# First stage of a two-layer SSM and mixture-of-experts kernel: one stored row per token, a skewed loop over pairs of tiles, and three engines in written order

## The chip, the cores and the metric

The kernel runs on one core of one Trainium2 chip. The metric is the device time of one launch in microseconds; the kernel before took 2048.63 us, the median of three runs from 2046.37 to 2051.86. The profile is that of one more execution, taken by the hardware profiler. Its engines are TensorE (PE, with its weight loads as PEld), VectorE (DVE), ScalarE (ACT), GpSimd (POOL) and SyncE (SP, which here only issues DMAs).

## The reference

The input `x` has 8 sequences of 1024 tokens of width 256, all in float32. Two layers follow, each of the form "x plus mixer of the normalized x plus experts of the normalized x":

```python
xn = layernorm(x)
x = x + attn0(xn) + ffn0(xn)      # attn0: scan h = A h + B x_t, y = C h + D x, layernorm, gelu, @ W_out.T + b_out, + xn
xn = layernorm(x)
x = x + attn1(xn) + ffn1(xn)      # attn1: softmax over an axis of length one; ffn1: 8 experts with a capacity

# ffn0, for each token
scores = sigmoid(xn @ router_weight.T)                 # 8 experts in 2 groups
masked = (scores + correction_bias) in the better group, 0 elsewhere
e1, e2 = top 2 of masked;  w1, w2 = scores[e1], scores[e2], divided by their sum
routed = w1 * expert_e1(xn) + w2 * expert_e2(xn)       # (silu(xn @ gate) * (xn @ up)) @ down, inner width 128
shared = (silu(xn @ sw_gate) * (xn @ sw_up)) @ sw_down
ffn0 = routed + shared
```

The change concerns the normalization, the shared expert and the routing of the first layer, and the rows that its routed experts read and write.

## The kernel before, in words

The 8192 tokens are 64 tiles of 128 tokens (one token per partition), 8 tiles per sequence. All of `x` lies in SBUF in the tile `y`. The program is written in a tile framework: a planner orders the instructions of every engine from dependencies, written order and modelled times, and adds the waits. Each engine then runs its own queue strictly in the planned order.

**First stage.** It goes over pairs of tiles, 32 pairs, in five sets of 8, 16, 16, 16 and 8 tiles. For a set, `scale` (L556) takes the square root of the variances on ScalarE (another activation table than the sigmoid's) and makes `rstd`, `off` and `up` on VectorE. For each tile, `measure` (L550) takes mean and variance on VectorE, one set ahead, and `normal` (L571) writes the normalized rows into `xr4` on VectorE, a ring of three buffers of four tiles each. After every fourth tile, two DMAs store these rows in DRAM, in `xnd`, which has **two rows per token**, one for each of its two experts: 256 values and, in column 256, the gate of that choice.

For each pair, `shared` (L596) lets TensorE turn the rows (`pair_turned`, four transposes, L249, copied by ScalarE at L253), makes the router's products (L606), and computes the shared expert: `hidden` (gate and up products, L263; sigmoid on ScalarE, L268; two products on VectorE, L270 and L271) and `down` (L278). `both` (L586) makes on ScalarE the copy `xc` for the scan (L588) and x plus xn in place in `y` (L592). VectorE adds the shared result to `y` (L617). In before all of one pair is written one after the other. Two steps of `krylov(0)`, which makes powers of the scan's matrix for four groups of channels (`begin`, then seven `level`; L322 on TensorE, copies L329 and L333), are written behind each pair until its eight steps are done.

Per sequence, `fill` (L533) writes the bias `b_out` into the DRAM tensor `base` from SP, and a DMA of POOL then accumulates `y` into it (L655). After every second sequence, `route0` (L482) makes the routing of 16 tiles: 33 small VectorE instructions one after the other, and two DMAs that store the gates (L528).

**After it.** A short part counts each expert's tokens (L671 to L724). Then come the scan and, woven into it, `find`/`found` (which token stands where in the experts' lists) and 71 expert blocks of 256 rows: `bring` gathers rows of `xnd` by an indirect DMA and the weights, `widen` turns them and computes `hidden`, `narrow` (L806) computes `down`, scales each row by its gate (L811) and scatters it into `yr`, two rows per token. The next part reads `base` and both `yr` rows of each token and adds them (`load`, L942), projects, normalizes, and makes the second layer, whose experts fill the second half of the time.

These lines set the first stage's order in before:

```python
for k in range(0, len(g), 2):
    for i in g[k + 4 : k + 6]:
        normal(i, ...)
    for i in nxt[k * len(nxt) // len(g) : (k + 2) * len(nxt) // len(g)]:
        measure(i, ...)
    ...
    shared(i, pr, rstd[:, k : k + 2])
    for step in steps[:2]:
        step()
```

Of the kernel before, what the change touches and what calls it, by code (L numbers as in the profile page):

```python
# [9 lines left out]
F32 = mybir.dt.float32  # L10
# [8 lines left out]
P = 128  # L19
EPS = 1e-5  # L20
BIG = 3.0e38


@with_exitstack
def kernel(
# [47 lines left out]
    NCOL = NBLK * BLK // P  # L73
    XW = D + 8
# [10 lines left out]
    kscr = dram.tile([D, 2 * P], F32, name="kscr")  # L85
    base = dram.tile([NTOK, D], F32, name="base")

    xnd = dram.tile([2 * NTOK, D + 1], F32, name="xnd")
# [109 lines left out]
    def pick_two(pool, v, n, hot, val):  # L198


        for k in range(2):
# [6 lines left out]
            nc.vector.tensor_reduce(first, cand, AX.X, ALU.max)  # L208
            oh = hot[k]
            nc.vector.tensor_tensor(oh, cand, bc(first, 2, [P, n, E]), ALU.is_equal)  # L210
            if k == 0:
                rest = pool.tile([P, n, E], F32, name="rest")
                nc.vector.scalar_tensor_tensor(rest, oh, -BIG, v, ALU.mult, ALU.add)
                v = rest


    with tc.tile_pool(name="xpool", bufs=1) as xpool, tc.tile_pool(name="mo", bufs=2) as mo, tc.tile_pool(
# [12 lines left out]
        g0 = xpool.tile([P, 2, NT], F32, name="g0")  # L230
        up = xpool.tile([P, NT], F32, name="up")
        off = xpool.tile([P, NT], F32, name="off")
# [4 lines left out]

        choice = xpool.tile([P, NCOL], I32, name="choice")
        goes = xpool.tile([P, NCOL], I32, name="goes")
# [16 lines left out]
        def hidden(xT, wb, pgu=None):  # L256
# [10 lines left out]
            sg = mo.tile([P, 2 * P], F32, name="sg")  # L267
            nc.scalar.activation(sg, pgu[:, 0, :], AF.Sigmoid)  # L268
            hh = mo.tile([P, 2 * P], F32, name="hh")
            nc.vector.tensor_tensor(hh, pgu[:, 0, :], sg, ALU.mult)  # L270
# [183 lines left out]
        with tc.tile_pool(name="sh", bufs=1) as sh, tc.tile_pool(name="ld", bufs=2) as ld, tc.tile_pool(  # L454
# [5 lines left out]
            scores = sh.tile([P, NT, E], F32, name="scores")  # L460
            cb_t = sh.tile([P, E], F32, name="cb_t")
# [10 lines left out]
            bout_t = sh.tile([P, D], F32, name="bout_t")  # L472
            nc.scalar.dma_start(bout_t, b_out.partition_broadcast(P))
# [6 lines left out]
            nc.vector.tensor_copy(rwT.rearrange("p c e -> p (c e)"), pr[:, : DC * E])  # L480

            def route0(n, tiles):  # L482
# [8 lines left out]
                nc.vector.tensor_tensor(lo, v[:, :, 0:2], v[:, :, 2:4], ALU.min)  # L491
                gs = rt.tile([P, 2 * n], F32, name="gs")
                nc.vector.tensor_reduce(gs, lo, AX.X, ALU.max)
                top = rt.tile([P, 2 * n], F32, name="top")
                nc.vector.tensor_reduce(top, hi, AX.X, ALU.min)
                nc.vector.tensor_tensor(gs, gs, top, ALU.max)
                nc.vector.tensor_reduce(top, hi, AX.X, ALU.max)
                nc.vector.tensor_tensor(gs, gs, top, ALU.add)
                gs2 = gs.rearrange("p (t g) -> p t g", g=2)
                gm = rt.tile([P, n, 2], F32, name="gm")  # L500
                nc.vector.tensor_tensor(gm[:, :, 0], gs2[:, :, 0], gs2[:, :, 1], ALU.is_ge)
                nc.vector.tensor_tensor(gm[:, :, 1], gs2[:, :, 1], gs2[:, :, 0], ALU.is_gt)
                masked = rt.tile([P, n, E], F32, name="masked")
# [7 lines left out]
                pick_two(rt, masked, n, hot, [rt.tile([P, n], F32, name=f"top{j}") for j in range(2)])  # L511
                w = rt.tile([P, n, E], F32, name="w")
                nc.vector.tensor_tensor(hot0[:, tiles, :], hot[0], hot[1], ALU.add)
                nc.vector.tensor_copy(first0[:, tiles, :], hot[0])
                nc.vector.tensor_tensor(w, hot0[:, tiles, :], sc, ALU.mult)
                den = rt.tile([P, n], F32, name="den")
                nc.vector.tensor_reduce(den, w, AX.X, ALU.add)
                nc.vector.tensor_scalar(den, den, 1e-20, None, ALU.add)
                nc.vector.reciprocal(den, den)
                nc.vector.tensor_tensor(w, w, bc(den, 2, [P, n, E]), ALU.mult)  # L520
                for k in range(2):
                    wk = rt.tile([P, n, E], F32, name="wk")
                    nc.vector.tensor_tensor(wk, w, hot[k], ALU.mult)
                    nc.vector.tensor_reduce(g0[:, k, tiles], wk, AX.X, ALU.add)
                    mine = xnd[2 * tiles.start * P : 2 * tiles.stop * P, :].rearrange(
                        "(i p k) c -> k p i c", p=P, k=2
                    )[k]
                    nc.sync.dma_start(mine[:, :, D], g0[:, k, tiles])  # L528
# [4 lines left out]
            def fill(b):  # L533

                nc.sync.dma_start(
                    base[b * S : (b + 1) * S, :].rearrange("(i p) d -> p i d", p=P),
                    bc(bout_t, 1, [P, TPB, D]),
                )

# [31 lines left out]
            def normal(i, mv, rstd):  # L571
# [7 lines left out]
                if i % 4 == 3:  # L579
                    for kk in range(2):  # L580
                        mine = xnd[2 * (i - 3) * P : 2 * (i + 1) * P, :].rearrange(
                            "(i p k) c -> k p i c", p=P, k=2
                        )[kk]
                        nc.sync.dma_start(mine[:, :, :D], rows[i // 4])
# [10 lines left out]

            def shared(i, pr, rstd):  # L596


                n = i // 2
                pt = None  # L600
                if n % 3:
                    pt = ps_m.tile([P, 512], F32, name="pm").rearrange("p (c t) -> p c t", c=DC)
                xT = pair_turned(rows[i // 4][:, i % 4 : i % 4 + 2, :], pt)
# [11 lines left out]
                pgu = ps_k.tile([P, 2, 2 * P], F32, name="pk") if n % 2 else None  # L615
                pd = down(hidden(xT, sw, pgu), sw)
                nc.vector.tensor_tensor(y[:, i : i + 2, :], pd, y[:, i : i + 2, :], ALU.add)  # L617

# [7 lines left out]
            pr = None  # L626
            for s, g in enumerate(sets):
                mv = mvs[s]
                rstd = scale(g, mv)
                nxt = []  # L630
                if s + 1 < len(sets):
                    nxt = list(sets[s + 1])
                    mvs.append(ld.tile([P, len(nxt), 2], F32, name="mv"))
                for i in g[:4]:
                    normal(i, mv[:, i - g[0], 0:1], rstd[:, i - g[0] : i - g[0] + 1])
                for k in range(0, len(g), 2):
                    for i in g[k + 4 : k + 6]:
                        normal(i, mv[:, i - g[0], 0:1], rstd[:, i - g[0] : i - g[0] + 1])
                    for i in nxt[k * len(nxt) // len(g) : (k + 2) * len(nxt) // len(g)]:
                        measure(i, mvs[s + 1][:, i - nxt[0], :])  # L640
                    i = g[k]
                    if i % TPB == 0:
                        pr = ps_y.tile([P, TPB, E], F32, name="py")
                        fill(i // TPB)
                        if i // TPB >= NB - len(pack):
                            nc.sync.dma_start(*pack[i // TPB - NB + len(pack)])
                    shared(i, pr, rstd[:, k : k + 2])
                    for step in steps[:2]:
                        step()
                    steps = steps[2:]  # L650
                    if i % TPB == TPB - 2:
                        b = i // TPB
                        tiles = slice(b * TPB, (b + 1) * TPB)
                        nc.scalar.activation(scores[:, tiles, :], pr, AF.Sigmoid)
                        nc.gpsimd.dma_start(  # L655
                            base[b * S : (b + 1) * S, :].rearrange("(i p) d -> p i d", p=P),
                            y[:, tiles, :], accum_op=ALU.add,
                        )
# [807 lines left out]
```

## Time and profile before

| | us |
|---|---|
| median of the runs | 2048.63 |
| profiled execution | 2030.81 |
| its span in the trace | 2029.1 |
| TensorE busy | 1825.1 |
| VectorE busy | 697.3 |
| ScalarE busy | 716.2 |
| GpSimd busy | 670.8 |
| mean granted TensorE clock | 0.952 of full speed |

The page's slices cut the span into 40 equal parts of about 51 us. A digit is the busy share in tenths, PEclk the clock granted to TensorE in tenths of full speed, DMA the mean busy share of the 16 DMA engines. In a list in order of time, a row begins with start and duration in us; "x8" means that eight instructions are merged; a bracket tells how long the engine was idle before and what released it. In a list of waits the numbers are the total in us, how many times, and the longest.

### The profile page before, as it was taken

To read this page: it belongs to the slowest core of one execution; us is meant where nothing else is said; L and a number is where in the kernel's file an instruction comes from. 1 tells how busy PE (TensorE), PEld (TensorE's weight loads), DVE (VectorE), ACT (ScalarE), POOL (GpSimd) and SP (SyncE) were. 2 spreads that over 40 slices of the span, in tenths; PEclk is the share of its full clock that TensorE was granted. 3 is DMA by queue.
4 is the path that set the end of the run, shared out by engine and by line. 5 is a ranking of instruction groups with operands and counts; after the bars stand their busy time and mean duration, and the time that the engine had idled before them with its cause. 6 is when DMAs were issued, how large, how long until landed. Compare 5 with 4: busy or idle time off the path is not lost.

```text
span 2029.1 us, 24196 instructions
## 1 busy us (share of the span) xinstructions
PE 1825.1 (90%) x8619; PEld 1379.9 (68%) x8619; DVE 697.3 (34%) x2101; ACT 716.2 (35%) x1626; POOL 670.8 (33%) x680
## 2 busy tenths in 40 slices
PE   6988798989898888748995999999999999999996
PEld 5866576877777776537973666666666666666664
DVE  6764795444453434437775111001000110001010
ACT  5963353232222222337982222222222222222221
POOL 0000002555555546411112333333333333333312
PEclk9988899999999999868997999999999999999998
DMA  9999313555454545499995223232323222232211
GB/s 267 222 199 201 49 54 115 151 149 152 146 164 138 146 130 170 122 281 253 224 237 128 38 60 61 42 72 39 82 39 73 41 61 57 57 59 38 40 18 21
DMA packets 228888, 233.16 MB, mean 115 GB/s; under 512 B 50904, under 2 KB 203296, under 8 KB 228640
## 3 DMA queue, kind: packets, MB, share of 16 engines
q0 software_dynamic: 69408, 102.87, 26.2%
q1 hardware_dynamic: 156672, 126.35, 22.5%
q10 hardware_dynamic: 2688, 2.40, 0.4%
q8 instruction: 68, 1.11, 0.2%
q14 instruction: 52, 0.43, 0.1%
HBM read 136.87 MB, written 97.85 MB: 116 GB/s over the span
## 4 chain that ended last, share of the span: by engine, by line
PE 48%; DMA 4%; issue 2%; DVE 2%; ACT 1%; POOL 1%; POOLq 0%; SPq 0%; DVEq 0%; ACTq 0%
PE phe L1393 22%; PE poe L1411 21%; DMA hb<-yr 2%; PE px L1376 1%; PE pd L996 1%; PE pd L1061 1%; DMA hb<-base 1%; PE pt L933 1%; DMA out_dram<-yo,invi 1%; PE pi L1162 0%; PE pt L1206 0%; PE pt L1042 0%; DVE y L1003 0%; DVE st L178 0%; POOL out_dram L1085 0%
## 5 line engine op out<-in xcount | busy, mean ns | idle before, releaser
L1393 PE MATMUL phe<-xTe,w1t 128*128 128x512 f32 x1024 | 447.1, 595 | 0.6 <-issue 0.6
L1411 PE MATMUL poe<-w2t,hT 128*128 128x256 f32 x2048 | 447.3, 379 | 0.0
L1411 PEld LDWEIGHTS poe<-w2t,hT 128*128 128x128 f32 x2048 | 386.7, 190 | 51.7 <-issue 0.5
L1393 PEld LDWEIGHTS phe<-xTe,w1t 128*128 128x128 f32 x1024 | 195.4, 191 | 233.6 <-issue 230.5
L1423 POOL DMA_INDIRECT out_dram<-yo,invi x128 | 201.6, 1575 | 447.7 <-DMA out_dram<-yo,invi 257.2
L1400 ACT ACTIVATE hT<-phe,b1T 128x512 f32<-128x512 f32 x256 | 175.9, 687 | 248.3 <-PE phe L1393 241.4
L1422 ACT ACTIVATE yo<-yo,gr 128x256 f32<-128x256 f32 x128 | 58.0, 500 | 441.4 <-DVE yo L1418 441.4
L1418 DVE TENSOR_TENSOR yo<-poe,b2t 128x512 f32<-128x512 f32 x64 | 44.2, 691 | 406.6 <-PE poe L1411 406.6
L1362 POOL DMA_INDIRECT xg<-xd,invi x128 | 124.0, 969 | 163.8 <-PE px L1376 125.8
L322 PE MATMUL pk<-kr 128*128 128x129 f32 (+7 forms) x896 | 151.4, 306 | 29.4 <-ACT kr L333 23.8
L1377 DVE COPY xTe<-px 128x512 f32<-128x512 f32 x64 | 41.2, 685 | 383.3 <-PE px L1376 383.2
L322 PEld LDWEIGHTS pk<-kr 128*128 128x128 f32 x896 | 130.1, 202 | 52.9 <-ACT kr L333 34.5
L814 POOL DMA_INDIRECT yr<-yo,goes x142 | 140.7, 990 | 76.7 <-DVE yo L811 35.2
L792 POOL DMA_INDIRECT xb<-xnd,choice x142 | 139.1, 980 | 46.9 <-issue 33.5
L263 PE MATMUL pgu<-xT,wb 128*128 128x256 f32 x568 | 144.2, 399 | 8.9 <-ACT xT L253 7.6
L263 PEld LDWEIGHTS pgu<-xT,wb 128*128 128x128 f32 x568 | 110.3, 200 | 37.4 <-ACT xT L253 18.5
L333 ACT COPY kr<-pk 128x256 f32<-128x256 f32 x192 | 69.6, 374 | 123.4 <-DVE kr L329 103.5
L268 ACT ACTIVATE sg<-pgu 128x256 f32<-128x256 f32 x87 | 33.3, 383 | 199.7 <-PE pgu L263 139.3
L278 PE MATMUL pd<-wb,hh 128*128 128x256 f32 x284 | 86.4, 421 | 11.4 <-DVE hh L271 7.6
L787 POOL COPY wb<-wrow 1x1 int32<-1x1 int32 x71 | 12.8, 180 | 234.4 <-PE pgu L752 117.5
L270 DVE TENSOR_TENSOR hh<-pgu,sg 128x256 f32<-128x256 f32 x87 | 36.8, 423 | 138.8 <-ACT sg L268 116.1
L996 PE MATMUL pd<-woutT,gT 128*128 128x256 f32 x256 | 63.5, 404 | 22.1 <-DVE y L1003 22.1
(322 smaller groups left out, 2375.3 us busy)
## 6 DMA issues: line engine op xcount, KB each, us to landing
wb<-wpk SPq DMA_DIRECT2D x71, 384.0 KB
xnd<-xr SPq DMA_DIRECT2D x32, 512.0 KB
hk<-kscr SPq DMA_DIRECT2D x32, 512.0 KB
hb<-yr POOLq DMA_DIRECT2D x14, 1024.0 KB
base<-bout_t SPq DMA_DIRECT2D x8, 1024.0 KB
base<-y POOLq DMA_DIRECT2D x8, 1024.0 KB
hb<-base SPq DMA_DIRECT2D x8, 1024.0 KB
w1t<-in_L_ffn_w_dram SPq DMA_DIRECT2D x8, 1024.0 KB
```

What stands on the lines that cost most here:

```text
L263: nc.tensor.matmul(pgu[:, j, :], lhsT=gu[:, j, c, :], rhs=xT[:, c, :], start=(c == 0), stop=(c == DC - 1),)
L278: nc.tensor.matmul(pd[:, q, :], lhsT=hh[:, q * P : (q + 1) * P], rhs=wb[:, 2 * DC * I : WW], start=True, stop=True,)
L322: nc.tensor.matmul(pk[:, j, :n], lhsT=t[:, 1 - j, P:], rhs=t[:, j, P - k : P - k + n], start=True, stop=True,)
L333: nc.scalar.copy(t[:, :, P:], pk[:, :, k : k + P])
L792: nc.gpsimd.indirect_dma_start(out=xb[:, q, : D + 1], out_offset=None, in_=xnd[:, :], in_offset=bass.IndirectOffsetOnAxis(ap=choice[:, 2 * ...
L814: nc.gpsimd.indirect_dma_start(out=next(yr_own)[:, :], out_offset=bass.IndirectOffsetOnAxis(ap=goes[:, 2 * n + q : 2 * n + q + 1], axis=0) ...
L996: nc.tensor.matmul(po[:, q, :], lhsT=gT[:, c, (t + q) * P : (t + q + 1) * P], rhs=woutT[:, c, :], start=(c == 0), stop=(c == DC - 1),)
L1362: nc.gpsimd.indirect_dma_start(out=xg[:, q, :], out_offset=None, in_=xd[:, :], in_offset=bass.IndirectOffsetOnAxis(ap=invi[:, q0 + q : q0 ...
L1393: nc.tensor.matmul(ph, lhsT=w1t[:, c, h * P : (h + 1) * P], rhs=xT[:, c], start=(c == 0), stop=(c == DC - 1),)
L1400: nc.scalar.activation(hT[:, h], ph, AF.Relu, bias=b1T[:, e * HC + h : e * HC + h + 1])
L1411: nc.tensor.matmul(po[:, r, :], lhsT=hT[:, h, q + r, :], rhs=w2t[:, h, :], start=(h == 0), stop=(h == HC - 1),)
L1423: nc.gpsimd.indirect_dma_start(out=of[:, :], out_offset=bass.IndirectOffsetOnAxis(ap=invi[:, q0 + r : q0 + r + 1], axis=0), in_=yo[:, r, : ...
```

## The change

It has five parts.

1. `xnd` has one row per token, of 258 values: the normalized row and both gates (`XR = D + 2`). One DMA instead of two stores four tiles of rows, and one instead of two the gates. The list `choice` holds token numbers, and a new tile `which` holds for each place of the lists a 1 at the choice that it is.
2. `base` is written once, from SP, with `y` after the shared result has been added, four tiles at a time; the fills and the accumulating DMAs are gone. The bias is loaded once, halved (`bhalf`), and added in `narrow` to both expert rows of each token; `narrow` picks the gate with `which`.
3. Pairs are skewed: the next pair is turned before the current one's router and hidden products, and `down` and the add of a pair come behind the hidden products of the next one. One Krylov step is written behind every second pair.
4. `route0` is a generator of 13 pieces, three of which are written behind each pair; it is called for 16, 16, 16, 8 and 8 tiles.
5. The loop stands in a block in which TensorE, VectorE and ScalarE keep the written order. `begin(s + 1)`, the scale of the next set and its first four `normal`, is written at the last pair of a set.

`hidden` also writes the sigmoid straight into `hh`, which has three buffers.

```diff
-    xnd = dram.tile([2 * NTOK, D + 1], F32, name="xnd")
+    xnd = dram.tile([NTOK, XR], F32, name="xnd")
...
+        bhalf = xpool.tile([P, D], F32, name="bhalf")
+        nc.scalar.dma_start(bhalf, b_out.partition_broadcast(P))
+        nc.scalar.mul(bhalf, bhalf, 0.5)
...
-            sg = mo.tile([P, 2 * P], F32, name="sg")
-            nc.scalar.activation(sg, pgu[:, 0, :], AF.Sigmoid)
-            hh = mo.tile([P, 2 * P], F32, name="hh")
-            nc.vector.tensor_tensor(hh, pgu[:, 0, :], sg, ALU.mult)
+            hh = mo.tile([P, 2 * P], F32, name="hh", bufs=3)
+            nc.scalar.activation(hh, pgu[:, 0, :], AF.Sigmoid)
+            nc.vector.tensor_tensor(hh, pgu[:, 0, :], hh, ALU.mult)
...
-                    for kk in range(2):
-                        mine = xnd[2 * (i - 3) * P : 2 * (i + 1) * P, :].rearrange(
-                            "(i p k) c -> k p i c", p=P, k=2
-                        )[kk]
-                        nc.sync.dma_start(mine[:, :, :D], rows[i // 4])
+                    mine = token_rows(slice(i - 3, i + 1))
+                    nc.sync.dma_start(mine[:, :, :D], rows[i // 4])
...
+                if i % TPB == TPB - 2:
+                    nc.scalar.activation(
+                        scores[:, i - TPB + 2 : i + 2, :], pr, AF.Sigmoid
+                    )
+                pgu = ps_k.tile([P, 2, 2 * P], F32, name="pk") if i // 2 % 2 else None
+                return hidden(xT, sw, pgu)
+
+            def add_shared(i, hh):
+
+                pd = down(hh, sw)
                 nc.vector.tensor_tensor(y[:, i : i + 2, :], pd, y[:, i : i + 2, :], ALU.add)
+                if i % 4 == 2:
+                    nc.sync.dma_start(
+                        base[(i - 2) * P : (i + 2) * P, :].rearrange("(i p) d -> p i d", p=P),
+                        y[:, i - 2 : i + 2, :],
+                    )
...
+            def begin(s):
+
+                g, mv = sets[s], mvs[s]
                 rstd = scale(g, mv)
+                for i in g:
+                    scale_of[i] = mv[:, i - g[0], 0:1], rstd, i - g[0]
                 for i in g[:4]:
+                    normal(i, scale_of[i][0], rstd[:, i - g[0] : i - g[0] + 1])
+
+            with tc.manual_schedule(engines=IN_ORDER):
+                begin(0)
+                turn(0)
+                pr, back = None, None
+
+                routes = {2 * TPB: 0, 4 * TPB: 2 * TPB, 6 * TPB: 4 * TPB, 7 * TPB: 6 * TPB, 8 * TPB: 7 * TPB}
+                routing = iter(())
+                for s, g in enumerate(sets):
+                    nxt = []
+                    if s + 1 < len(sets):
+                        nxt = list(sets[s + 1])
+                        mvs.append(ld.tile([P, len(nxt), 2], F32, name="mv"))
+                    for k in range(0, len(g), 2):
+                        for i in g[k + 4 : k + 6]:
+                            mean, rstd, j = scale_of[i]
+                            normal(i, mean, rstd[:, j : j + 1])
+                        for i in nxt[k * len(nxt) // len(g) : (k + 2) * len(nxt) // len(g)]:
+                            measure(i, mvs[s + 1][:, i - nxt[0], :])
+                        if nxt and k == len(g) - 2:
+                            begin(s + 1)
+                        i = g[k]
...
+                        if i + 2 < NT:
+                            turn(i + 2)
+                        rstd = scale_of[i][1]
+                        hh = shared(i, pr, rstd[:, k : k + 2])
+                        if back:
+                            add_shared(*back)
+                        back = i, hh
+                        if i // 2 % 2 and steps:
+                            steps.pop(0)()
+                        for _ in range(3):
+                            next(routing, None)
+                        if i + 2 in routes:
+                            for _ in routing:
+                                pass
+                            routing = route0(i + 2 - routes[i + 2], slice(routes[i + 2], i + 2))
+                add_shared(*back)
+                for _ in routing:
+                    pass
...
+                gk = mo.tile([P, 2, 2], F32, name="gk")
+                tc.keep_in_program_order(nc.vector.tensor_tensor(
+                    gk, xb[:, :, D:XR], which[:, 2 * n : 2 * n + 2, :], ALU.mult
+                ))
+                gs = mo.tile([P, 2], F32, name="gs")
+                nc.vector.tensor_reduce(gs, gk, AX.X, ALU.add)
...
-                    nc.vector.tensor_scalar(
-                        yo[:, q, :], pd[:, q, :], xb[:, q, D : D + 1], None, ALU.mult
+                    nc.vector.scalar_tensor_tensor(
+                        yo[:, q, :], pd[:, q, :], gs[:, q : q + 1], bhalf, ALU.mult, ALU.add
                     )
```

## The prediction

> **What bounds the kernel now.** I read the page's slices first, then the windows, then the first 260 us by waits and in order of time. Four rows of the slices (51 us each):
>
> ```profile
> PE   6988798989898888748995999999999999999996
> ...
> DVE  6764795444453434437775111001000110001010
> ...
> PEclk9988899999999999868997999999999999999998
> DMA  9999313555454545499995223232323222232211
> ```
>
> From 330 us on TensorE is the bound (454.6 us busy of 525 between 330 and 855 us, then nearly all of the span to the end), and the change leaves that work alone but for some VectorE instructions. What it rewrites is the first four slices: DMA full, TensorE not. So the question is when the first stage ends. In before, the last shared result is added (L617) at 202.6 us and the last routing instruction (L524) ends at 210.1; the position counts (L674 on) need it. The waits of the SP queue in the first 260 us:
>
> ```profile
> SPq L528 <- DVE g L524: 32.6, 2, 22.5
> SPq L584 <- DVE xr L576: 24.8, 3, 8.6
> ```
>
> (total us, times, longest.) The queue that must store `xr` rows stood behind a gate store that waited for a whole routing. VectorE and TensorE at the worst place, in order of time:
>
> ```profile
> 156.80 0.28 DVE L524 TENSOR_REDUCE g<-wk 128x16 f32<-128x128 f32 x1
> 157.00 1.37 DVE L576 TENSOR_SCALAR xr<-y,mv,rstd 128x256 f32<-128x256 f32 x4
> ...
> 157.46 0.80 PE L249 MATMUL pt<-ident,xr 128*128 128x128 f32 x2 [7.00 <-DVE xr L576]
> ```
>
> All 33 routing instructions had run (145.75 to 157.00) before the `normal` (L576) that TensorE needed: 7.0 us idle. Another gap is at the change to the last set of tiles; windows of TensorE alone (busy, clock, DMA share, GB/s):
>
> ```profile
> 120.00:124.00 4.00, 2.16 (x11) 1.00 0.68 74
> 124.00:128.00 4.00, 1.80 (x4) 0.71 0.93 68
> 128.00:132.00 4.00, 3.05 (x13) 0.50 0.99 300
> 132.00:136.00 4.00, 4.00 (x13) 0.51 1.09 317
> 136.00:140.00 4.00, 4.00 (x26) 1.00 1.16 191
> ```
>
> Here TensorE waited 3.2, 1.1 and 0.7 us for the square root, `normal` and copy of the new set, and worked at clock 0.50 from 125.4 to 136. Nine busy us at half speed lose 4.6; with 5.0 idle, this set change cost 9.6 us. Pairs 5 to 19 otherwise ran at 3.9 us (L617 from 72.3 to 127.2 us), pairs 20 to 31 at 6.3.
>
> **DMA, part by part.** Removed: half of the `xr` stores (16 of 32, 8.4 MB), eight fills of `base` (8.4 MB), eight accumulating stores on POOL (now 16 plain stores on SP, the same 8.4 MB), four of eight gate stores. 48 MB in the first 260 us becomes about 31. At the 240 GB/s of 40 to 100 us that is 130 us of transfer in a stage of 200, so I take DMA off the path; SP also issues less (eight fills at 1.3 us, sixteen stores at 1.0, against sixteen new at 1.0), and what it waits for now all comes from one VectorE order, so no store stands ahead of an earlier one. Price on the path: nothing, gain: what the written order lets through. If that cover is gone, the 12 late pairs lose 2.4 us each again (6.3 less 3.9): 29 us.
>
> **TensorE in written order.** Starts of neighbouring instructions at full clock give each step's cost: turn 0.43 (191.07 to 191.50), router 0.81 (175.77 to 176.58), hidden 1.81 (173.96 to 175.77), down 0.87 (190.20 to 191.07): 3.92 a pair, 32 pairs 125.4 us. The queue can start the router when the router weights are turned (L480, 18.9 us); in before it started at 22.98 because VectorE came late to L562. The first 8 us run at half clock, as in before: 4.
>
> **Krylov steps.** One after every second pair, eight in all. L322 takes about 0.55 a group (1.1 to 1.3 for eight instructions, two groups, between 45 and 53 us): 2.2 for four. `pk` has two buffers, so group three waits for the copies of group one, which stand behind `hh` (0.46 + 0.34) and the add (0.61) on VectorE: about 1.0. 8 x 3.2 = 25.6. In before other pairs covered these waits.
>
> **Set changes.** `begin(s+1)` stands ahead of `turn(i+2)` in the last pair of a set, and its first `normal` feeds that turn, so nothing on TensorE can pass it. VectorE gets to it late: add of the pair before (1.4 us behind TensorE), three routing pieces (2.0: 8.7 us for 33 instructions, 13 pieces), then two measures 0.87, square root and its two hops 0.4, reciprocal, `off`, `up` 0.55, two `normal` 0.75. That is 6.0 us of idle TensorE at pairs 11, 19 and 27, and 4.9 at pair 3 (no pieces, four measures). Behind it are queued router, hidden and down of that pair, and everything later. Each gap is over the 3.2 us after which the windows above show half clock, and those 9 us cost 4.6 more; the table load (1.28, row L268) before the next sigmoid lies mostly beside it. Sum 9.5 to 10.6; the gap measured in before gave 9.6. I take 10, four times: 40 us. From both sides: nothing, if it hides; 14, if the clock stays down for 12.5 us (157.5 to 170) and the reload delays `hh`.
>
> The Trainium skill, "TensorE: Matmul & The Clock Gate", Part 1, says that an idle window of about 3.4 us halves the clock and that about 3.4 us of busy time restores it. The first half agrees with the row; the second does not (9 busy us here). By the page a set change would lose 1.7 instead of 4.6 and the forecast would be 12 us lower; I go by the rows.
>
> **VectorE and ScalarE.** A pair costs VectorE 0.67 + 0.87 + 0.80 + 0.61 = 3.0 us and pieces 2.0 in about half of the pairs; ScalarE 1.43 + 1.0 + 0.5 + 0.35 = 3.3. Both are below 3.92 on average and the skew lets them lag by a pair, so I charge nothing; if the lag were not absorbed, 12 pairs x 1.1 = 13 us.
>
> **End of the stage.** 18.9 + 4 + 125.4 + 25.6 + 40 = 213.9; last down and add 2.0; the last routing, eight tiles, begins after that add with 33 instructions of 0.2: 6.6. Together 222.5 against 210.1: 12.4 us later. Before began the second Krylov chain inside this stage (L307 at 199.25); behind the written block it can't be that early in relation to the end: 5 us (from 0 to 10, the 10 us by which it preceded the end).
>
> **Expert blocks.** Each of 71 `narrow` gets two tiny VectorE instructions, about 0.16 each by the small rows (L501, L518), 23 us in all, and two scalar_tensor_tensor for two tensor_scalar (0.476, L811; the nearest two-input row, L270, is 0.42). VectorE is busy 222.8 of 525 us there and `yo` is needed a block (7.4 us) later, so 2 us, between -5 (the gate is read earlier, which frees `xb`; `sg` is gone) and +23. `found` gains an instruction or two: nothing. The halved bias, one ScalarE instruction on 256 columns: nothing.
>
> Sum 12.4 + 5 + 2 = 19.4 us. The profiled execution took 2030.81 us (span 2029.1 and 1.7 around it), 17.8 below the median of the runs, 2048.63; the profile after should span about 2048 and the median be 2048.6 + 19.4 = 2068.
>
> **Rivals.**
> - *Faster: the set changes hide.* If order of writing turns out not to bind at `begin` (or VectorE is ahead by then), the 40 us go and the stage ends at 182.5: 27.4 earlier, less 7 for the rest: 2028. It decides at 5 us a set change, half of the price: below that the kernel is faster. For it: before crossed three of its four set changes without a TensorE wait over 1.2 us, and the 7.0 us gap and the 22.5 us queue wait vanish. Against: in before a planner moved other pairs in there, which the written order forbids. Chance 0.30.
> - *Nothing measurable.* Stalls of half price (5 us), or savings on DMA that just pay for them: about 2048. 0.3% is about what a measurement of this kernel can tell from no change. Chance 0.08.
> - *Slower still: the tail too.* The 23 us of gate instructions, pinned behind what was traced before them, do reach TensorE (70 of 525 us idle there already), or a set change costs 14: 2084 to 2091. Chance 0.14.
> - *Forecast*, 2068, within 2052 to 2082. Chance 0.48.
>
> **How the numbers follow.** Slower is 0.48 + 0.14 = 0.62, same 0.08, faster 0.30. The range goes from 2022 (the faster case with 6 us to spare) to 2092 (the worst bounds); the likeliest case alone is 2052 to 2082. What is left outside is some 0.08 at each end.
>
> **What would show it.** Right: four gaps of 4 to 7 us on TensorE before L249 of tiles 8, 24, 40 and 56, released by `normal` or the copy, each followed by windows at clock 0.50; DMA share near 0.6 in the stage; SP waits without 22 us entries; last L617-type add at about 216 us, last routing instruction at about 222; stores of `base` on SP; later stages of the same length. Wrong: set changes without gaps, an end of routing before 200 us, TensorE gaps at every Krylov step, or a block stage longer or shorter than 525 us by over 5.

## The result and the profile after

The kernel after took 2074.18 us (median of four runs, 2069.01 to 2079.61), the kernel before 2050.24 (four runs, 2046.37 to 2053.43): a ratio of 1.012 with the 95% interval 1.0094 to 1.0145. So the change makes the kernel 23.9 us slower in these runs, where 2068 was forecast. The profiled execution of after took 2079.61 us (span 2077.9). The four rows of the slices that were shown of before:

```profile
PE   4788799888888887765896899999999999999997
...
DVE  4666797443434443353869011001011001010100
PEclk8988899989999999887998899999999999999999
DMA  8233223444445445559999223232322222232211
```

In the first four slices (208 us) DMA has gone from 9 to 2 and 3 after the first slice, and TensorE is no busier for it. SP's waits in the first 260 us:

```profile
SPq L639 <- DVE y L637: 122.8, 16, 14.0
SPq L593 <- DVE xr L588: 20.4, 5, 5.4
SPq L547 <- DVE g L546: 13.8, 2, 7.4
```

SP now waits in the order in which VectorE works: its 16 stores of `base` for the add, which nobody needs in this stage. The 22.5 us behind a gate store are gone. TensorE's long gaps, in order of time (from the list of TensorE alone):

```profile
46.32 1.23 PE L260 MATMUL pm<-ident,xr 128*128 128x128 f32 x4 [4.50 <-DVE xr L588]
...
101.95 1.22 PE L260 MATMUL pt<-ident,xr 128*128 128x128 f32 x4 [6.66 <-DVE xr L588]
...
154.62 1.23 PE L260 MATMUL pm<-ident,xr 128*128 128x128 f32 x4 [7.56 <-DVE xr L588]
...
195.18 1.23 PE L260 MATMUL pm<-ident,xr 128*128 128x128 f32 x4 [6.03 <-DVE xr L588]
```

These are the four set changes, at tiles 8, 24, 40 and 56: the turn (L260, before's L249) waits for the first `normal` of the set (L588). VectorE before the third of them:

```profile
148.97 0.68 DVE L637 TENSOR_TENSOR y<-pd,y 128x512 f32<-128x512 f32 x1
149.56 0.28 DVE L218 TENSOR_TENSOR oh<-cand,first 128x128 f32<-128x128 f32 x1
...
152.16 0.42 DVE L565 BATCH_NORM_STATS2 st<-y 128x6 f32<-128x256 f32 x1
...
153.71 0.25 DVE L574 RECIPROCAL rstd<-rstd 128x16 f32<-128x16 f32 x1 [0.38 <-ACT rstd L573]
...
154.16 1.38 DVE L588 TENSOR_SCALAR xr<-y,mv,rstd 128x256 f32<-128x256 f32 x4
```

It is the queue that the prediction listed: the add of the pair before, three routing pieces (149.56 to 152.2), two measures, the scale, `normal`. In all of it VectorE shows one wait, of 0.38 us. Behind the gap the clock is down (windows of TensorE alone: busy, clock, DMA share, GB/s):

```profile
150.00:154.00 4.00, 0.00 (x0) 0.50 0.37 131
154.00:158.00 4.00, 3.38 (x14) 0.50 0.39 130
158.00:162.00 4.00, 4.00 (x18) 0.73 0.02 5
162.00:166.00 4.00, 4.00 (x27) 1.00 0.00 0
```

At 0.73 in the window from 158, full speed came back at about 160: some 5.5 us of work at half clock.

Where the time went, stretch by stretch, with the same table for two chips on which the expert blocks ran shorter (before is the run e9_before_look, after e8_after_again, below):

| stretch | predicted | the two executions profiled first | e9 to e8 |
|---|---|---|---|
| start to the last routing instruction | +12.4 | 209.87 to 231.35: +21.5 | 209.9 to 229.8: +19.9 |
| from there to the first row gathered for the experts | +5 | 118.0 to 113.5: -4.5 | 118.0 to 113.5: -4.5 |
| expert blocks, first gather to last scatter | +2 | 527.4 to 561.5: +34.1 | 462.7 to 450.7: -12.0 |
| from there to the second layer's first gather | 0 | 237.3 to 236.8: -0.5 | 235.6 to 232.9: -2.7 |
| the rest | 0 | 936.6 to 934.8: -1.8 | 937.4 to 934.2: -3.2 |
| sum | +19.4 | +48.8 | -2.5 |

The profiled execution of before lies 19.4 us below the median of its runs, that of after 5.4 above: of the 48.8 only 23.9 hold for the medians. (That of before need not be from the same chip.) All stretches but the expert blocks differ by under 3 us between the two columns, so I put the other 24.9 in the blocks; their share is then about +9 by the medians. That is inferred, not measured.

### The profile page after: what moved, and what is told of

Same layout as the page of the kernel before. It is cut to its first block, busy times and chain, and to the rows that moved or that the text cites. A ratio compares the mean times of both kernels' runs of the same rounds, so it can differ in the third digit from the quotient of the medians.

```text
span 2077.9 us, 24352 instructions
## 1 busy us (share of the span) xinstructions
PE 1835.9 (88%) x8619; PEld 1389.5 (67%) x8619; DVE 724.3 (35%) x2277; ACT 731.8 (35%) x1628; POOL 663.8 (32%) x672
## 4 chain that ended last, share of the span: by engine, by line
PE 49%; DMA 3%; DVE 3%; ACT 1%; issue 1%; POOL 0%; POOLq 0%; SPq 0%; DVEq 0%; ACTq 0%
PE phe L1448 21%; PE poe L1466 21%; PE pd L1051 2%; DMA hb<-yr 2%; PE px L1431 1%; PE pt L988 1%; PE pd L1116 1%; DMA hb<-base 1%; DMA out_dram<-yo,invi 1%; DVE hh L1207 0%; DVE hl L1202 0%; PE pt L1097 0%; PE pi L1217 0%; PE pt L1261 0%; PE pc L1134 0%
## 5 line engine op out<-in xcount | busy, mean ns | idle before, releaser
L332 PE MATMUL pk<-kr 128*128 128x129 f32 (+7 forms) x896 | 152.7, 308 | 37.2 <-ACT kr L343 29.4
L332 PEld LDWEIGHTS pk<-kr 128*128 128x128 f32 x896 | 131.1, 203 | 61.7 <-ACT kr L343 40.1
L279 ACT ACTIVATE hh<-pgu 128x256 f32<-128x256 f32 x87 | 33.1, 381 | 209.3 <-PE pgu L274 110.1
L280 DVE TENSOR_TENSOR hh<-pgu,hh 128x256 f32<-128x256 f32 x87 | 36.8, 423 | 148.1 <-ACT hh L279 117.4
L866 DVE SCALAR_TENSOR_TENSOR yo<-pd,gs,bhalf 128x256 f32<-128x256 f32 x142 | 62.1, 479 | 61.3 <-PE pd L288 39.2
```

The source lines that it names most:

```text
L332: nc.tensor.matmul(pk[:, j, :n], lhsT=t[:, 1 - j, P:], rhs=t[:, j, P - k : P - k + n], start=True, stop=True,)
L866: nc.vector.scalar_tensor_tensor(yo[:, q, :], pd[:, q, :], gs[:, q : q + 1], bhalf, ALU.mult, ALU.add)
```

## The experiments

The experiments ran on four chips. Before took 2033.19 and 2050.52 us on two of them, 1967.34 and 1968.98 on the other two, so times are compared within a chip. On the first two, and in the runs of the result, the profiles show TensorE's results coming late in the expert blocks (last experiment); I call these late chips and the other two prompt ones.

**e1_early_begin** (late chip): the scale of the next set and its first four `normal` one pair (two tiles) earlier, and its measures to match. The expectations of e10 and e11 below call the same edit two pairs earlier; it is one.

```diff
-  for i in nxt[k * len(nxt) // len(g) : (k + 2) * len(nxt) // len(g)]:
+  for i in nxt[k * len(nxt) // (len(g) - 4) : (k + 2) * len(nxt) // (len(g) - 4)]:
...
-  if nxt and k == len(g) - 2:
+  if nxt and k == len(g) - 4:
```

> After, with the next set's scale and first four `normal` written one pair earlier and its measures finished before that. Theory (the four set changes are the cost): the gaps of 4.5 to 7.6 us before the turn of tiles 8, 24, 40 and 56 go, and with them the half clock behind each; the last routing instruction moves from 231 us to about 195, and the whole takes 30 to 40 us less than after, about 2038. Rival (VectorE's lag only shows elsewhere): new TensorE waits of about the same sum appear at the Krylov steps or the hidden products, and the last routing instruction ends at 220 or later, less than 12 us gained.

Measured: 2044.75 us against 2033.19, ratio 1.0059 (1.0035 to 1.0084). The last routing instruction starts at 209.4 us, 22 earlier than in after, 21 earlier than in e4 below, which has after's loop on this chip (230.2), and where before has it. TensorE's waits from 20 to 215 us (total, times, longest):

```profile
PE pk L332 <- DVE hh L281: 8.1, 7, 2.0
...
PE pm L260 <- DVE xr L588: 3.1, 3, 1.4
...
PE pt L260 <- DVE xr L588: 1.4, 1, 1.4
```

The waits for `normal` fall from 24.9 us to 4.5, and the stage ends 22 us earlier: that much of the 38.7 that the pairs lose around set changes (next section) can be had by writing the same work sooner. Part of the rest shows as waits for other work of VectorE (`hh`, 8.1 here and 4.2 in after). The kernel is still slower than before, with a first stage as long: something lies behind it.

**e2_planner** (same chip): the skewed loop and the pieces, but no written order.

```diff
-            with tc.manual_schedule(engines=IN_ORDER):
+            if True:
```

> After without the block of written order: the planner orders all engines, everything else as in after. Theory (written order costs): no TensorE wait on `normal` over 3 us but perhaps one at the last set, last routing instruction before 205 us, 25 us less than after. Rival (the skew and the pieces are what costs, in whatever order): the end of the stage stays within 8 us of after's 231.

Measured: 2046.40 us, 1.0063 (1.0036 to 1.0091); last routing instruction at 207.9. From 20 to 210 us:

```profile
PE pt L260 <- DVE xr L588: 9.2, 3, 7.1
PE pm L260 <- DVE xr L588: 5.3, 1, 5.3
```

The planner keeps gaps of 5 and 7 us at set changes too, yet ends the stage 23 us earlier than the written order (22 earlier than e4 on this chip). The waits for `normal` sum to 14.5 us, where after has 24.9, and those inside Krylov steps (`PE pk L332`) to 1.5 us, where after has 6.5 up to 215 us. That is 15 of the 23; the rest wasn't taken apart. So the skew and the pieces alone don't lengthen the stage.

**e3_rows_only** (same chip): one row per token, `base` stored once, half of the bias in each expert row, with the loop of before.

```diff
-            with tc.manual_schedule(engines=IN_ORDER):
-                begin(0)
...
+            for s, g in enumerate(sets):
+                begin(s)
...
+                    turn(i)
+                    add_shared(i, shared(i, pr, scale_of[i][1][:, k : k + 2]))
+                    for step in steps[:2]:
+                        step()
...
+                    if i % (2 * TPB) == 2 * TPB - 2:
+                        for _ in route0(2 * TPB, slice(i + 2 - 2 * TPB, i + 2)):
+                            pass
```

> Parts 1 and 2 alone (one row per token, base stored once, halved bias, gate by `which`) with the loop of before in the planner's order: no skew, routing in one go for 16 tiles, two Krylov steps behind each pair. If DMA held up the late pairs in before, as the prediction priced it: last routing instruction at about 185 us against 210. If order held them up (routing ahead of `normal`): at 205 to 212. The expert blocks (first gather to last scatter) took 527 us in before and 561 in after: about 530 if the gate instructions are covered, as predicted, and about 560 if they are what lengthens the blocks.

Measured: 2057.78 us, 1.0122 (1.0099 to 1.0144); last routing instruction at 214.6. Two windows, the first stage of before and of this kernel, the last two columns DMA share and GB/s:

```profile
20.00:210.00 190.00, 169.16 (x933) 0.93 0.96 227
```

```profile
20.00:215.00 195.00, 171.04 (x937) 148.83 (x937) 125.56 (x463) 125.69 (x261) 0.00 (x0) 0.89 0.44 139
```

The DMA share falls from 0.96 to 0.44 and the bytes from 43 MB to 27 (GB/s times the window), and no time is gained: DMA was full in before's first stage, but it didn't set its end. TensorE waits twice for `normal`, 6.7 and 7.0 us, the second time behind a whole routing as in before. The expert blocks took 550.2 us, nearer to the 560 expected if the gate instructions lengthen them than to 530.

**e4_no_pin** (same chip): `gk`, the product of gates and `which`, may be planned anywhere.

```diff
-                tc.keep_in_program_order(nc.vector.tensor_tensor(
+                nc.vector.tensor_tensor(
                     gk, xb[:, :, D:XR], which[:, 2 * n : 2 * n + 2, :], ALU.mult
-                ))
+                )
```

> After without the pin on the gate product in `narrow`, so that the planner may place it. If the pin holds the gathers back (GpSimd waits 47 us for `gs` in after): expert blocks of about 530 us instead of 561, 25 to 30 us less than after. If the longer blocks come from the instructions themselves or from this one execution: within 6 us of after. First stage as in after either way, last routing instruction at about 231.

Measured: 2088.43 us, 1.0264 (1.0239 to 1.0290). That is 43.7 above e1 on the same chip: the first stage, which is after's here, accounts for 20.8 (230.2 and 209.4), the expert blocks for 18.5 (577.5 and 559.0). Without the pin the blocks are longer, not shorter, so it is not what lengthens them.

**e5_no_gate_ops, e6_two_rows, e7_half_steps, e8_after_again** (a prompt chip, before 1967.34). The first three start from e1. e5 drops the two gate instructions; its rows are scaled by the first gate, so the choice of the gate is left out:

```diff
-                gk = mo.tile([P, 2, 2], F32, name="gk")
...
-                nc.vector.tensor_reduce(gs, gk, AX.X, ALU.add)
...
-                        yo[:, q, :], pd[:, q, :], gs[:, q : q + 1], bhalf, ALU.mult, ALU.add
+                        yo[:, q, :], pd[:, q, :], xb[:, q, D : D + 1], bhalf, ALU.mult, ALU.add
```

> The early-begin variant without the two gate instructions of `narrow`: every row is scaled by its token's first gate, so the choice between the two gates is left out; everything else, the gather of one row per token and the halved bias too, stays. The expert blocks took 559 us with them and 527 in before. Theory (the two instructions, in the chain between gather, `yo` and the next gather, are what lengthens the blocks): about 530 us, 25 to 30 us less in all. Rival (the gather from one row per token, the two-input `yo` or the sigmoid written into `hh` does it): within 8 us of 559.

e6 goes back to two rows per token, with the gate in the row, and so needs no gate instructions either:

```diff
-    xnd = dram.tile([NTOK, XR], F32, name="xnd")
+    xnd = dram.tile([2 * NTOK, D + 1], F32, name="xnd")
...
-                        out=xb[:, q, :XR],
+                        out=xb[:, q, : D + 1],
```

> The early-begin variant with two rows per token in `xnd` again, each with its gate, as in before; base stored once, halved bias, skew, pieces and written order stay. If the doubled row stores hurt in the written order: last routing instruction later than 209 us by 5 or more. If DMA has room, as the run with the rows alone suggests: within 3 us of 209. Expert blocks: as without the gate instructions if those are the cause (about 530 us), shorter than that run by over 8 us if both experts' reading of one row costs. Whole: about 2020, faster than before by 0.5% or so, if both hold.

e7 splits each Krylov step into two halves of two groups, one behind each of the first 16 pairs:

```diff
+                two = groups[:2], groups[2:]
+                return [lambda h=h: begin(h) for h in two] + [
+                    lambda k=k, h=h: level(k, h) for k in (1, 2, 4, 8, 16, 32, 64) for h in two
+                ]
...
-                        if i // 2 % 2 and steps:
+                        if steps:
```

> The early-begin variant with every Krylov step cut into two halves of two groups, one half behind each of the first 16 pairs, so that no half needs a third buffer. The waits in Krylov steps (8.1 us on `hh` and 3.3 on copies, 11.4 in all) should fall to under 4 us and the last routing instruction should come at about 202 us instead of 209. Rival: VectorE, not these waits, sets the rate of the pairs; then waits on `normal` take their place and the end stays within 3 us of 209. Blocks as in the early-begin variant, about 559 us.

e8 is after, unchanged.

> The changed kernel once more, beside the others on one chip. If the profiled after was typical: last routing instruction at 231 us, expert blocks at 561 us, ratio to before about 1.012 to 1.02. If its long blocks belonged to that one execution: blocks below 550 us.

Measured, with the stage ends from their profiles:

| run | median us | ratio | last routing | expert blocks |
|---|---|---|---|---|
| e5_no_gate_ops | 1946.90 | 0.9900 (0.9872 to 0.9927) | 208.5 | 454.5 |
| e6_two_rows | 1952.86 | 0.9936 (0.9916 to 0.9957) | 209.1 | 460.4 |
| e7_half_steps | 1949.69 | 0.9911 (0.9884 to 0.9939) | 212.3 | 452.9 |
| e8_after_again | 1969.17 | 1.0013 (0.9997 to 1.0030) | 229.8 | 450.7 |

Three things follow. After itself is hardly slower than before here, although its first stage ends as late as in the first profile: some 20 us come back behind it. Halving the Krylov steps gained nothing: pairs with a half step take 4.8 to 5.0 and 6.7 us by turns, 3.7 to 3.9 above two bare pairs together, as a whole step does (3.7), and the stage ended 3 us later than in e1. And one row per token is worth 6 us in the blocks (e5 beside e6). TensorE's wait for gathered rows in the blocks, first e6, then e5, then e7, which has the gate instructions:

```profile
PE pt L259 <- DMA xb<-xnd,choice: 19.6, 17, 2.5
```

```profile
PE pt L260 <- DMA xb<-xnd,choice: 16.3, 16, 3.4
```

```profile
PE pt L260 <- DMA xb<-xnd,choice: 8.0, 5, 3.5
```

**e9_before_look** and **e10_two_rows_again** (the other prompt chip, before 1968.98). e9 is before, unchanged, e10 is e6.

> The kernel before, unchanged, for a profile on the chip that the next run shares. Two chips have given the same kernel different expert blocks: 561.5 us of after on one, 450.7 us on the other, with the first stage the same to 2 us (last routing 231.3 and 229.8). If the change lengthens the blocks by itself, by work that reaches TensorE, the blocks of before are shorter than those of after on either chip: about 525 beside 561, or about 420 beside 451. If what lengthens them is on some chips only (TensorE results that come late), before shows 525 to 530 on a chip of the first kind, and on a chip of the second kind 445 to 470, no shorter than after's 451: there the 2.6 us between the two medians would be the 20 us of the first stage less some 17 from the later stages. The first stage ends at 208 to 211 us either way.

> The change with the next set begun two pairs earlier, two rows per token with the gate in the row, and no gate instructions in the expert blocks; half of the bias is still added to each row. Theory that the gate instructions lengthen the blocks: on a chip of the first kind blocks of 525 to 535 us, as before has them there (527.4), beside 559 with the gate instructions, and a total 25 to 35 us shorter than that kernel's, so a ratio of 0.985 to 0.995. Theory that the new shape of the blocks as a whole, or the earlier stages' order, does it: 550 to 560, ratio about 1.005. On a chip of the second kind 460 us and 0.994 as measured there once.

Measured: e9 1965.47 us (0.9985, 0.9974 to 0.9997, a kernel against itself, and 1 lies outside: a difference of 0.2% is not to be trusted here), blocks 462.7, last routing instruction 209.9. e10 1952.54 us, 0.9906 (0.9886 to 0.9926), blocks 462.1. With before's profile the table above closes for the prompt chips: after's blocks are 12.0 us shorter there, which pays most of the 19.9 of the first stage. The wait for gathered rows in the blocks, first before (e9), then after (e8):

```profile
PE pt L249 <- DMA xb<-xnd,choice: 19.7, 16, 3.5
```

```profile
PE pt L260 <- DMA xb<-xnd,choice: 7.2, 4, 3.1
```

In after the first of the two gate instructions reads the gates from `xb` ahead of the scaling, and nothing later needs `xb`. Step by step on the prompt chips: blocks of 462.7 us in before, 460.4 and 462.1 with two rows and the new `narrow` (e6 and e10, one kernel on two chips), 454.5 with one row (e5), and with the gate instructions 452.9 (e7) and 450.7 (e8, whose first stage is another). So the new `narrow` by itself shows nothing beyond the 1.7 us between e6 and e10, the single row about 6, the early read of the gates 1.6 to 3.8.

**e11_early_again** and **e12_no_gate_ops_again** (a late chip, before 2050.52): e1 and e5 side by side.

> The change with the next set begun two pairs earlier, now on a third group of chips. If the chip shows TensorE's results on time in the expert blocks (before's blocks 462.7 us there), the stages add up: first stage 209 to 210 us (as before), blocks 450 to 453 (12 us shorter, since the gate instructions let the rows of a later block be gathered earlier: waits of TensorE for gathered rows 7 to 8 us beside 19.7 in before), later stages 2 us less: a ratio of 0.987 to 0.991. If the results come late there (before's blocks 527), blocks of 555 to 562 and a ratio of 1.003 to 1.009, as on the first of these chips.

> The same without the two gate instructions in each narrow: the rows are scaled by the first gate, and the choice between the two gates is left out. Where TensorE's results are on time: blocks of 454 to 456 and waits for gathered rows of 16 us, since a row buffer is free only after the scaling: 2 to 4 us slower than the run beside it. Where they are late, the theory that the gate instructions are what makes the blocks of after 34 us longer than before's expects 525 to 535; the theory that it comes from the one row per token or the shape of the blocks expects 550 to 560.

Measured: e11 2058.38 us, 1.0032 (1.0011 to 1.0054), blocks 558.8. e12 2032.35 us, 0.9895 (0.9852 to 0.9938), blocks 544.7. So on a late chip the two gate instructions cost 26 us by the medians (18.2 by the profiled executions, 14.0 of these in the blocks), while their own time is some 20 us of VectorE. The 544.7 lies between the ranges of both theories (525 to 535, 550 to 560): without the gate instructions these blocks are still 17 us longer than the 527.4 of before's profile. No profile of before is known to be from this chip, so whether something else in the change lengthens them on late chips is open. The windows of the blocks (busy us of TensorE, weight loads, VectorE, ScalarE, GpSimd; then clock, DMA share and GB/s), e11, then e12:

```profile
323.50:882.20 558.70, 468.60 (x2582) 393.68 (x2581) 239.51 (x798) 137.58 (x362) 295.32 (x351) 0.92 0.47 138
```

```profile
321.50:866.30 544.80, 465.02 (x2579) 388.75 (x2578) 225.74 (x656) 135.15 (x357) 292.83 (x352) 0.93 0.49 142
```

TensorE is idle for 90 and 80 us of these; in e8, on a prompt chip, for 20 of 450.7. What a late result looks like: in after, TensorE issues the gate and up products of a block and two later products, and ScalarE's sigmoid starts late.

```profile
448.39 1.89 PE L274 MATMUL pgu<-xT,wb 128*128 128x256 f32 x8
450.12 0.91 PE L390 MATMUL pm<-xc,vT 128*128 128x448 f32 x2
```

```profile
453.07 0.39 ACT L279 ACTIVATE hh<-pgu 128x256 f32<-128x256 f32 x1 [4.33 <-PE pk L332]
```

```profile
454.50 0.62 DVE L394 TENSOR_TENSOR sm<-pm,mask 128x448 f32<-128x448 f32 x1 [0.59 <-remote]
```

The products end by the record at 450.28; the sigmoid that needs only them starts 2.8 us later, and VectorE's use of the L390 products at 454.50, 3.5 us after they end. (The profile models the ends of matmuls, so it can't tell a result that was late from news of it that was late.) The same place in e8:

```profile
428.92 1.89 PE L274 MATMUL pgu<-xT,wb 128*128 128x256 f32 x8
```

```profile
430.85 0.38 ACT L279 ACTIVATE hh<-pgu 128x256 f32<-128x256 f32 x1 [1.58 <-PE pgu L274]
```

Here it starts 0.04 us after their end. Of 71 blocks, the sigmoid starts over 1 us after the issue of the last product in 6 blocks of before, 18 of after, 17 of e11 and 9 of e12 on late chips, and in none on the prompt ones. In after TensorE then stands idle for over 1 us in 14 of the 18, and the clock falls to 0.50 behind 10. From the recorded ends on, the late sigmoids sum to 20 us in before and 44 in after, where these blocks are 65 and 111 us longer than those of e9 and e8: the rest, other late results and work at half clock among it, is not taken apart. They come at the same places: of the 15 blocks with a late sigmoid in e1, 10 are late in e11 on another chip and 13 in after, so the order of the program goes far to pick the places, and the chip decides whether they are stops. Why is open: eight gate and up products take 1.89 us on either kind of chip, and DMA is less busy on the late ones (0.47 beside 0.58). DMA packets of the two queues that the profile calls instruction don't single the late blocks out either: in after they fall into the wait or the 2 us ahead of it in 7 of the 18, and into a stretch of that mean length in 20 of the 53 others. That there are more late blocks with the gate instructions is what one execution of each shows (17 in e11, 9 in e12); how it comes about is not shown.

## Why the prediction was right, step by step

The forecast, 2068 within 2052 to 2082, holds the 2074.18. Its first-stage mechanism was right, with smaller terms off; of its three other terms one was wrong in sign and one had no single value. That the sum came within 5 us (+23.9 for +19.4) is partly luck: the stage ended 9 us later than worked out, the stretch behind it was 9.5 shorter than charged, the blocks took about 7 more (inferred) and the later stages 2.3 less. And it holds for the chips of these runs: in e8, on a prompt chip, after is within 0.3% of before, which is what the rival "nothing measurable" said, though for another reason. One sign of being wrong that was named, blocks off 525 us by over 5, did appear (561.5).

**DMA off the path: right.** The share in the stage is 0.42 (20 to 230 us), where about 0.6 was expected, no 22-us wait of SP is left, and e3 shows that lifting the DMA load alone gains nothing.

**Set changes, 40 us: right.** From the starts of the router products, the two pairs around each change take 21.3, 20.7, 18.4 and 17.0 us; less two pairs of 3.92 each, and less a Krylov step of 3.7 in the first two, that is 9.8, 9.2, 10.5 and 9.2: 38.7. The division was a little different: the gaps are 24.8 where 22.9 was summed, and half clock costs less than 4.6 each time. It held for about 8, 7, 5.5 and 6 us of work behind the four gaps, not nine, which is 2.8 to 4 us lost. (The 3.2 us of before's row, put down to the square root, ended with `hh`, L271: its sigmoid started at 123.94, behind the square root and two table loads from 121.03 on.) "TensorE: Matmul & The Clock Gate", Part 1 of the Trainium skill gives about 3.4 us; the runs lie between the page and the row that I used.

**Pairs, 3.92 us: right.** Between set changes and without a Krylov step the router products follow each other by exactly that.

**Krylov steps, 25.6: too small.** Five pairs with an undisturbed step lie 3.34 to 4.27 above 3.92, 3.7 on average: 29.3. In these five the waits sum to 1.2 us a step where 1.0 was charged, and the products take 2.5 where 2.2 was. e7 shows that cutting a step in two doesn't make it cheaper.

**Start, 18.9: too early.** The router begins at 21.6 us: the turn of its weights starts at 19.52, when their DMA has landed (18.30 in before), and two turns of rows at half clock stand between. With the half-clock start shorter (2.7 for 4) this is +1.4.

**Last pair and routing, 2.0 and 6.6: too small.** The last add starts 8.6 us after the last router (5.9 expected), since the planner put the start of the second Krylov chain (L317 at 217.06) between the last hidden and the last `down`; and from there to the end of the last routing instruction it took 8.5. In sum the stage ended 9 us later than the 222.5 of the working: 21.5 for 12.4.

**Second Krylov chain later, 5: wrong.** It starts 14.3 us before the last routing instruction, in before it was 10.4 (L307 starts at 199.47 there, not 199.25); the stretch to the first gather became 4.5 us shorter. The step that failed: "behind the written block it can't be that early". The block orders what is written in it; instructions traced behind it were moved in between.

**Expert blocks, 2, from -5 to 23.** The bounds were nearly the right two ends, but not as an uncertainty of one value: on prompt chips -12.0, of which "the gate is read earlier, which frees `xb`" is 2 to 4 (priced at 5 at most), and 6 are the single row, which the working gave no price in the blocks; on the late chips the 23 us of gate instructions do reach TensorE (26 by e11 and e12), less what the rows gain. In the runs of the result that left about +9 by the medians. The rival "slower still" was right in this part on late chips; its other condition, 14 us a set change, didn't come.

**The faster rival** needed set changes under 5 us; they cost 9.7 (its 27.4 is 27.6, 40 less 12.4). What would become of it is e1: on the prompt chips its variants e5 (without the choice of the gate), e6 and e7 are 0.6 to 1.0% faster than before, on the late ones it is itself 0.3 to 0.6% slower. No complete version here is shown to beat before on both kinds. e6 and e10, two rows and no gate instructions, do it on the prompt chips (0.9936 and 0.9906); on a late chip they weren't run, and e12's 0.9895, without the choice of the gate, only suggests that they would.

## What to carry to other kernels

When three engines are made to keep written order, go through the slowest one's queue at each change of phase and add up what stands ahead of the instruction that another engine waits for: the four gaps here came out of that list to 2 us in 25. Write the hand-over a step earlier, as e1 does, rather than where the loop happens to end. And a small instruction added to an inner loop has no fixed price: the same two instructions freed a buffer earlier on one chip (waits for gathered rows of 8.0 us beside 16.3) and cost 26 us by the medians, for some 20 of their own, on another, so compare on more than one chip before trusting a difference of 1%.

## What the runs showed of the hardware

- Before took 1967 to 1969 us on two chips and 2033 to 2050 on others, and in the two profiles the difference is in one stage: the last routing instruction starts at 209.9 us in both, the blocks take 462.7 and 527.4.
- On the slower chips the sigmoid of 6 to 18 of 71 blocks started 1.0 to 5.9 us after the issue of the last product that it needs, at places that repeat from chip to chip (10 of 15 blocks of one kernel on two chips); on the two faster chips in no block.
- In after the 7.56 us gap of TensorE was followed by 5.5 us of work at clock 0.50, the shorter gap of 4.50 us at 46 us by about 8.
- Taking a stage's DMA share from 0.96 to 0.44 (before, e3) didn't shorten it: 209.9 and 214.6 us to the last routing instruction.
